# A block projection in forty-two steps instead of eighteen: the turn of queries and keys, one GpSimd operation a step

## The chip, the cores and the metric

The kernel runs on one core of a Trainium2 chip. The metric is the device time of one execution in microseconds. The core's engines are TensorE (PE: matrix products and transposes; PEld: its weight loads), VectorE (DVE), ScalarE (ACT), GpSimd (POOL) and SyncE (SP, which here issues DMA transfers). Each engine works through its own instructions strictly in order and waits on semaphores for what others must deliver.

## The reference

A layer norm, causal attention with rotary positions, and a feed-forward network on the same normalised input whose output gates the attention:

```python
xn = _layernorm(x, axis=-1)                     # x: (4, 2048, 256)
q, k, v = (split(xn @ W.T + b) for W, b in ...) # 16 heads of 16
q = apply_rope(q); k = apply_rope(k)            # x * cos + rot(x) * sin
att = jnp.einsum('bhqd,bhkd->bhqk', q, k) / scale
att = jnp.where(mask, att, -jnp.inf)            # causal
y = softmax(att) @ v                            # per head, then joined
s = y @ Wo.T + bo
h = gelu(xn @ ternary(W1).T + b1)               # 1024 wide
g = silu(h @ ternary(W2).T + b2)
out = x + s * g
```

## The kernel before

The 4 x 2048 rows are cut into 16 *blocks* of 512 rows (`NB`), four to a sequence; `n = blk % 4` is a block's place in its sequence. For each block there are four stages: `project` (layer norm, transposes, queries, keys and values), `feed` (the feed-forward network), attention, and `finish` (output projection, gate, residual).

Attention goes over 64 *groups*: a block and four of its sixteen heads. Within a group the generator `values` runs over *units*, one for each 128 keys that the block may see, so a group has 4 (n + 1) units: 4, 8, 12 or 16. A unit computes scores on TensorE (L791), their exponential on ScalarE (L798) and the product with the values on TensorE (L815); the product of one unit is issued in the second half of the next. The last four units of a group lie on the diagonal: there GpSimd zeroes the masked triangle with two selects (L802), and the value product waits for them. The value products of a group's last two units are issued only after the first unit of the next group (`end`). `maxima` computes the row maxima of the *next* group (L704 on TensorE, L727 and L731 on VectorE) between the units of this one.

The order of instructions on every engine is written out by hand: the main loop (L1092 to L1146) calls these generators in turn, and each engine's queue holds what was issued in that order. Side work goes between the units. A generator is wrapped in `Paced`, which knows how many steps it has and, called with a share, runs as many as this share asks for. After each unit the loop advances the projection of a later block:

```python
proj, p0, p1 = Paced(project(b2), [1] * N_Q), g, g + over   # L1105
proj.to(1.05 * (g + (u + 1) / units - p0) / (p1 - p0))       # L1137
```

So a projection is spread over two groups. Which block is projected where says `beside` (L1053): while n = 1 or 2 is attended, the next block is projected in groups 0 and 1; while n = 3 is attended, the next block in groups 0 and 1 and the one after in groups 2 and 3; while n = 0, none. Blocks 0 and 1 are projected during the start (`start` is true for them, and VectorE does their arithmetic in place of GpSimd); the other fourteen are projected as described. Before a block is fed (`feed`, begun in the middle of the group ahead of the one named in `hids`) its projection is finished in one go if it isn't yet (`proj.rest()`, L1133). `feed` starts with four GpSimd operations on the transposed input (`split`, L572), and its `hl` differences (L594) are GpSimd's too.

The steps of `project`, each ended by a `yield`, are before the change: four steps of statistics on VectorE (L411, L412), of which the fourth also issues the normalisation on GpSimd (L419 to L432 on four columns, then L444 and L447 on the whole block); three more steps with nothing in them; two steps of four transposes (L455) and a copy (L458); then the query pair in two steps (two matmuls at L513 and an activation at L521 each), the key pair likewise, four steps of value products (L539, L548), and the store of the values. With the first query step go the load of the next block's x (L402) and of the rotation table cos_sin (L470), both on SP. As soon as a pair stands, `turn` (L474) rotates it: six multiplications, additions and subtractions of 128 x 512, and two calls of `split` (L391), which write a number as a sum of a rounded part and a rest (two operations each). These ten operations, all on GpSimd, are issued in one go, ahead of the key pair's first matmul or, for the keys, ahead of the first value product; the four stores of a turned pair to DRAM (L502, on SP) follow them. The tiles `qkhi`, `qklo`, `r0`, `r1` and `cos_sin` exist once each, `qk0` and `qk1` twice. `N_Q` (L1038) counts the steps: 18.

Of the kernel before, what the change touches and what calls it, by code (L numbers as in the profile page):

```python
# [20 lines left out]
NB = 512  # L21
# [17 lines left out]
def attention_gated_by_ffn(  # L39
# [40 lines left out]
    NT = T // P  # L80
    QK = 2 * D
    PR = H // 2

    x_blk = x.rearrange("b (n t p) d -> (b n) p t d", t=TT, p=P)
    out_blk = out.rearrange("b (n t p) d -> (b n) p t d", t=TT, p=P)
# [305 lines left out]
    def split(hi, lo, full, width):  # L391

        z = zero
        for _ in width[1:]:
            z = z.unsqueeze(1)
        nc.gpsimd.tensor_tensor(hi, full, z.to_broadcast([P, *width]), ALU.add)  # L396
        nc.gpsimd.tensor_tensor(lo, full, hi.bitcast(F32), ALU.subtract)  # L397


    def load(blk):  # L400
# [3 lines left out]
    def project(blk):  # L404
# [12 lines left out]
        start = blk < 2  # L417
# [25 lines left out]
        else:  # L443
# [1 line left out]
                xn, xn, mv[:, :, 0:1].to_broadcast([P, TT, D]), ALU.subtract  # L445
            )
            eng.tensor_tensor(xn, xn, r.unsqueeze(2).to_broadcast([P, TT, D]), ALU.mult)  # L447
        for _ in range(4):
            yield

        xf = x_T[blk] = tp.tile([P, KC, NB], F32, tag="tT", name="xf")
# [22 lines left out]
        def turn(i, t0, t1):  # L474
            r0 = one.tile([P, NB], F32, tag="r0", name="r0")
            r1 = one.tile([P, NB], F32, tag="r1", name="r1")
            eng.tensor_tensor(r0, t0, cos, ALU.mult)
            eng.tensor_tensor(r1, t1, sin, ALU.mult)
            eng.tensor_tensor(r0, r0, r1, ALU.subtract)
            if not start:  # L480
                split(hi[:, 2 * i, :], lo[:, 2 * i, :], r0, (NB,))
            else:
                nc.scalar.copy(hi[:, 2 * i, :], r0)
            eng.tensor_tensor(t0, t0, sin, ALU.mult)
            eng.tensor_tensor(t1, t1, cos, ALU.mult)
            eng.tensor_tensor(t0, t0, t1, ALU.add)
            if not start:
                split(hi[:, 2 * i + 1, :], lo[:, 2 * i + 1, :], t0, (NB,))
            else:
                nc.scalar.copy(hi[:, 2 * i + 1, :], t0)  # L490
                for k, full in ((2 * i, r0), (2 * i + 1, t0)):
                    eng.tensor_tensor(
                        lo[:, k, :], full, hi[:, k, :].bitcast(F32), ALU.subtract
                    )

            dd, rows = ((qd, (hi, hi, lo, lo)), (kd, (hi, lo, hi, lo)))[i]
            for c, src in enumerate(rows):
                to = dd[blk].rearrange(
                    "r (a f s c) k -> c (r a f) s k", a=2, f=HF, s=2
                )  # L500
                queue = nc.scalar if blk == 0 and i == 1 else nc.sync
                queue.dma_start(  # L502
                    out=to[c], in_=src[:, 2 * i : 2 * i + 2, :].bitcast(F32)
                )

        pairs = []
        for i in range(2):
            pair = []
            for s in range(2):
                pq = bank("pq")  # L510
                for kc in range(KC):
                    at = (2 * i + s) * P
                    nc.tensor.matmul(  # L513
                        pq,
                        wqkvT[:, kc, at : at + P],
                        xf[:, kc, :],
                        start=(kc == 0),
                        stop=(kc == KC - 1),
                    )
                t = work.tile([P, NB], F32, tag=f"qk{s}", name=f"qk{s}")  # L520
                nc.scalar.activation(t, pq, AF.Identity, bias=bqk[:, i, s : s + 1])  # L521
                release("pq")
                pair.append(t)
                yield
            pairs.append((i, *pair))
            while pairs and (blk or i):
                turn(*pairs.pop(0))


        v = one.tile([P, TT, VW], F32, tag="v", name="v")  # L530
# [35 lines left out]
    def feed(blk):  # L566

        xf = x_T.pop(blk)
        xh = tp.tile([P, KC, NB], F32R, tag="tT", name="xh")
        xl = tp.tile([P, KC, NB], F32R, tag="tT", name="xl")  # L570
        for kc in range(KC):
            split(xh[:, kc, :], xl[:, kc, :], xf[:, kc, :], (NB,))  # L572
        yield
        gate = gs[blk] = work.tile([P, KC, NB], F32, tag="g", name=f"g_{blk}")
        pgs, halves = [bank(f"pg{dc}") for dc in range(KC)], {}
        for f in range(FC + 2):
            if f < FC:
                ph = bank("ph")
                for kc in range(KC):
                    for i, x12 in enumerate((xh, xl)):  # L580
                        nc.tensor.matmul(  # L581
                            ph,
                            w1T[:, kc, f * P : (f + 1) * P],
                            x12[:, kc, :],
                            start=(kc + i == 0),
                            stop=(kc + i == KC),
                        )
                h = work.tile([P, NB], F32, tag="h", name="h")
                hh = hp.tile([P, NB], F32R, tag="hh", name="hh")
                hl = hp.tile([P, NB], F32R, tag="hl", name="hl")  # L590
                for to in (hh, h):
                    nc.scalar.activation(to, ph, AF.Gelu, bias=b1c[:, f : f + 1])  # L592
                release("ph")
                nc.gpsimd.tensor_tensor(hl, h, hh.bitcast(F32), ALU.subtract)  # L594
                halves[f] = hh, hl
            yield
            if f >= 2:
                for dc in range(KC):
                    for i, hx in enumerate(halves[f - 2]):
                        nc.tensor.matmul(  # L600
                            pgs[dc],
                            w2T[:, f - 2, dc * P : (dc + 1) * P],
                            hx,
                            start=(f - 2 + i == 0),
                            stop=(f - 2 + i == FC),
                        )
        for dc in range(KC):
            nc.scalar.activation(  # L608
                gate[:, dc, :], pgs[dc], AF.Silu, bias=b2c[:, dc : dc + 1]
            )  # L610
            release(f"pg{dc}")
        yield
# [423 lines left out]
    CHUNK, BESIDE, SH, END = 200, 300, 0.5, -200  # L1036
    N_R = 1 + 2 * 2 * (NQ - 1) + 2 * (1 + 12)
    N_Q = TT - 1 + 4 + KC + 4 + TT + 1  # L1038
    idle = Paced(iter(()), ())

    def max_work(blk):
# [25 lines left out]
    with tc.manual_schedule():  # L1067
# [24 lines left out]
        for i, (blk, g) in enumerate(groups):  # L1092
            n = blk % NQ
            units = (n + 1) * TT
            loads.now = i
            loads.go()
            nxt = groups[i + 1] if i + 1 < len(groups) else None
            maxs = Paced(maxima(*nxt), max_work(nxt[0])) if nxt else idle
            projs, hids = beside(blk)
            if g in projs:  # L1100
                proj.rest()
                b2, over = projs[g]
                proj = idle
                if b2 < NBLK:
                    proj, p0, p1 = Paced(project(b2), [1] * N_Q), g, g + over  # L1105

            fast = hids.get(g, NBLK) < NBLK
            slots = [CHUNK] * FC if fast else []
            for u in range(units):
                w = NB - max(u - n * TT, 0) * P  # L1110
                w += 80 + (BESIDE if proj is not idle else 0)
                slots += [w * SH, w * (1 - SH)]
            whole = sum(slots[:-2]) - END
            past = 0
            if fast:
                for k, _ in enumerate(gate):
                    past += slots.pop(0) if k < FC else 0

                    if k % 3 == 2:
                        maxs.to(past / whole)  # L1120
            steps = values(blk, g)
            for u in range(units):
                past += slots.pop(0)
                maxs.to(past / whole)
                next(steps)
                past += slots.pop(0)
                maxs.to(past / whole)
                next(steps)
                if u == 0 and ends:
                    ends.pop(0)()  # L1130
                if u == units // 2 and hids.get(g + 1, NBLK) < NBLK:
                    if b2 == hids[g + 1]:
                        proj.rest()  # L1133
                    gate = feed(hids[g + 1])
                    next(gate)
                if proj is not idle:
                    proj.to(1.05 * (g + (u + 1) / units - p0) / (p1 - p0))  # L1137
                if deferred:
                    do = deferred.pop(0)
                    if do:  # L1140
                        do()
            for _ in steps:
                pass
            loads.release("q")
            maxs.rest()
            if g == G - 1:  # L1146
                proj.rest()
# [60 lines left out]
```

## Time and profile before

| | |
|---|---|
| median of 3 runs | 2407.71 us (2400.47 to 2412.79) |
| profiled execution, first to last instruction | 2397.2 us |
| instructions | 43912 |
| selects, L802, GpSimd | 512, 416 ns each, 208.0 us |
| differences of the feed-forward network, L594, GpSimd | 128, 1298 ns each, 164.9 us |
| one operation of a turn, GpSimd (ten rows, 28 of each) | 1041 to 1285 ns |
| normalisation of a whole block, L444 and L447, GpSimd | 1898 and 1895 ns |
| row maxima, L727, VectorE | 2048, 666 ns each, 1258.2 us |
| exponentials, L798, ScalarE | 1280, 894 ns each, 1081.3 us |

Times in the profile are microseconds from the first instruction of that execution unless ns is written. A row of a timeline has the start, the duration, the engine, the line of the kernel, the operation, what it writes and reads, the shape and a count of merged instructions; in square brackets stands how long the engine had been idle before it and what released it. A row of waits reads: who waited, for whom, microseconds in all, times, longest. A row of windows has the stretch, its length, the busy time of PE, PEld, DVE, ACT and POOL (with instructions), the clock granted to TensorE as a share of its full speed, the share of the DMA engines' time and GB/s. In the chain of waits, the profile follows the work that ended last back to what released it.

### The profile page before, as it was taken

Reading aid. Unit: us, or ns where it says so; the run is one execution under the profiler, and the core shown is the slowest. Engines: PE = TensorE matmul, PEld = TensorE weight load, DVE = VectorE, ACT = ScalarE, POOL = GpSimd, SP = SyncE. Lnnn points to the kernel's source line nnn. Section 1 sums busy time; section 2 is a strip of 40 time slices with the busy share of each in tenths; the row PEclk is TensorE's granted clock in tenths of the full one; section 3 lists DMA queues with packets and bytes.
Section 4 is the critical chain, followed back from the end, with each engine's and each line's share of the span. In section 5 each row is a group of like instructions: output and inputs, shape, how many; then the busy total and the mean of one; then the engine's idle time right before and its main releaser. Section 6 shows DMA issues by size and latency. Waiting matters only on the chain.

```text
span 2397.2 us, 43912 instructions
## 1 busy us (share of the span) xinstructions
PE 2269.8 (95%) x16852; PEld 1222.7 (51%) x16852; DVE 1620.1 (68%) x2910; ACT 1472.5 (61%) x1889; POOL 886.6 (37%) x1262
## 2 busy tenths in 40 slices
PE   5799999999999999999999999999999999999997
PEld 4554545545455455544545454455554545455443
DVE  9656677775556676696636768768663766777881
ACT  4554656656766565765766565565676646566665
POOL 2136343235443535315344542522525453431000
PEclk8889999999999999999999999999999999999998
DMA  7344335234253524234234443412514352442311
GB/s 222 113 135 161 92 127 157 58 104 136 75 165 118 178 86 159 79 91 145 67 127 128 151 142 111 155 56 86 176 58 140 120 179 79 135 140 62 88 46 32
DMA packets 247617, 280.38 MB, mean 117 GB/s; under 512 B 108784, under 2 KB 143728, under 8 KB 247408
## 3 DMA queue, kind: packets, MB, share of 16 engines
q1 hardware_dynamic: 243680, 271.95, 35.7%
q10 hardware_dynamic: 3728, 5.64, 0.7%
q8 instruction: 132, 2.16, 0.4%
q14 instruction: 77, 0.63, 0.1%
HBM read 181.08 MB, written 87.52 MB: 112 GB/s over the span
## 4 chain that ended last, share of the span: by engine, by line
PE 71%; DVE 10%; ACT 7%; POOL 6%; issue 3%; DMA 2%; SPq 1%; ACTq 0%; DVEq 0%; POOLq 0%
PE psum L791 19%; PE psum L815 19%; PE psum L704 14%; PE psum L600 5%; PE psum L513 3%; PE psum L581 3%; DVE mx L727 3%; ACT e L798 3%; DVE mx L731 2%; PE psum L539 2%; PE psum L953 2%; PE psum L717 2%; ACT mT L765 1%; POOL qklo L397 1%; ACT g L608 1%
## 5 line engine op out<-in xcount | busy, mean ns | idle before, releaser
L727 DVE TENSOR_REDUCE mx<-psum 128x1 f32<-128x512 f32 (+1 forms) x2048 | 1258.2, 666 | 497.1 <-PE psum L704 350.1
L798 ACT ACTIVATE e<-psum 128x1024 f32<-128x1024 f32 (+3 forms) x1280 | 1081.3, 894 | 630.4 <-PE psum L791 596.0
L704 PE MATMUL psum<-kst,qst 64*128 64x512 f32 (+3 forms) x2560 | 613.0, 421 | 27.1 <-ACT h L592 9.3
L815 PE MATMUL psum<-e,vg 128*32 128x512 f32 (+3 forms) x5120 | 596.5, 543 | 15.7 <-POOL e L802 15.5
L802 POOL TENSOR_SCALAR_AFFINE_SELECT e<-e 128x256 f32<-128x256 f32 x512 | 208.0, 416 | 1001.0 <-ACT e L798 972.2
L791 PE MATMUL psum<-qst,kst 64*128 64x512 f32 (+3 forms) x2560 | 554.6, 395 | 22.3 <-DVE mx L727 5.7
L704 PEld LDWEIGHTS psum<-kst,qst 64*128 64x128 f32 x2560 | 309.0, 185 | 449.4 <-DVE mx L727 287.9
L791 PE MATMUL psum<-mT,sel 64*128 64x512 f32 (+3 forms) x2560 | 516.8, 370 | 6.0 <-ACT mT L765 3.2
L791 PEld LDWEIGHTS psum<-qst,kst 64*128 64x128 f32 x2560 | 285.1, 185 | 171.9 <-ACT e L798 55.4
L791 PEld LDWEIGHTS psum<-mT,sel 64*128 64x128 f32 x2560 | 273.3, 186 | 43.7 <-ACT mT L765 24.1
L594 POOL TENSOR_TENSOR hl<-h,hh 128x512 fp32r<-128x512 f32 x128 | 164.9, 1298 | 149.9 <-ACT h L592 114.3
L815 PEld LDWEIGHTS psum<-e,vg 128*32 128x32 f32 x5120 | 109.9, 108 | 161.0 <-issue 112.4
L731 DVE TENSOR_REDUCE mx<-psum 128x3 f32<-128x384 f32 x256 | 130.3, 552 | 57.7 <-PE psum L717 53.3
L592 ACT ACTIVATE hh<-psum,b1c 128x512 fp32r<-128x512 f32 x128 | 88.4, 691 | 80.4 <-PE psum L581 80.2
L513 PE MATMUL psum<-xf,wqkvT 128*128 128x512 f32 x256 | 125.9, 616 | 0.9 <-ACT xf L458 0.9
L717 PE MATMUL psum<-mask_k,mask_q 64*128 64x64 bf16 (+1 forms) x1536 | 121.1, 205 | 0.0
L600 PE MATMUL psum<-hh,w2T 128*128 128x512 f32 x256 | 107.1, 418 | 0.2 <-ACT w2T L367 0.2
L581 PE MATMUL psum<-xh,w1T 128*128 128x512 f32 x256 | 104.8, 409 | 0.6 <-POOL xh L396 0.5
L581 PE MATMUL psum<-xl,w1T 128*128 128x512 f32 x256 | 103.1, 403 | 0.8 <-POOL xl L397 0.8
L600 PE MATMUL psum<-hl,w2T 128*128 128x512 f32 x256 | 102.3, 399 | 0.2
L521 ACT ACTIVATE qk<-psum,bqk 128x512 f32<-128x512 f32 x64 | 44.0, 689 | 86.4 <-PE psum L513 85.9
L592 ACT ACTIVATE h<-psum,b1c 128x512 f32<-128x512 f32 x128 | 87.9, 687 | 0.0
(135 smaller groups left out, 1635.9 us busy)
## 6 DMA issues: line engine op xcount, KB each, us to landing
kst<-kd SPq DMA_DIRECT2D x160, 512.0 KB
qst<-qd SPq DMA_DIRECT2D x64, 512.0 KB
vg<-vd SPq DMA_DIRECT2D x160, 166.0 KB
qd<-qkhi SPq DMA_DIRECT2D x32, 512.0 KB
qd<-qklo SPq DMA_DIRECT2D x32, 512.0 KB
kd<-qkhi SPq DMA_DIRECT2D x30, 512.0 KB
kd<-qklo SPq DMA_DIRECT2D x30, 512.0 KB
vd<-v SPq DMA_DIRECT2D x16, 574.0 KB
```

The lines of the kernel that those rows point to most:

```text
L513: nc.tensor.matmul(pq, wqkvT[:, kc, at : at + P], xf[:, kc, :], start=(kc == 0), stop=(kc == KC - 1),)
L581: nc.tensor.matmul(ph, w1T[:, kc, f * P : (f + 1) * P], x12[:, kc, :], start=(kc + i == 0), stop=(kc + i == KC),)
L592: nc.scalar.activation(to, ph, AF.Gelu, bias=b1c[:, f : f + 1])
L600: nc.tensor.matmul(pgs[dc], w2T[:, f - 2, dc * P : (dc + 1) * P], hx, start=(f - 2 + i == 0), stop=(f - 2 + i == FC),)
L704: nc.tensor.matmul(s1[:, at : at + wt], q[rows, j, t * P : (t + 1) * P], kst[blk, g, c][rows, j, :wt], start=(at == 0), stop=(c < n),)
L717: nc.tensor.matmul(to[:, :, i * ST : (i + 1) * ST], mask_q[rows, i, :], mask_k[rows, i, : len(ts), :], start=False, stop=(i == 1),)
L727: nc.vector.tensor_reduce(mx[:, 2 * j + a, at : at + 1], s1[:, :w], AX.X, ALU.max)
L731: nc.vector.tensor_reduce(mx[:, 2 * j + a, at : at + w // P], s1[:, :w].rearrange("p (b k) -> p b k", k=P), AX.X, ALU.max,)
L791: nc.tensor.matmul(s2[:, a, :w], (k, sels[j][rows, :])[part], (q[rows, j, q0:], mT[rows, q0:])[part], start=(part == 0), stop=(part == 1),)
L798: nc.scalar.activation(e, s2[:, :, :w], AF.Exp, scale=1.0 / math.sqrt(HD))
L802: nc.gpsimd.affine_select(out=e[:, :, :P], in_=e[:, :, :P], pattern=[[0, 2], [1, P]], compare_op=ALU.is_ge, fill=0.0, base=0, channel_mult ...
L815: nc.tensor.matmul(av[h * HP : (h + 1) * HP, q0:], vst[blk, g, kb // TT][:, kb % TT, h * VE : h * VE + HP], ex[h // 2][:, h % 2, : NB - q0 ...
```

## The change

`split` and `turn` become generators that yield after each operation, so a turn is issued in ten steps in place of one go; `feed` runs `split` through without a pause as before. At the start (blocks 0 and 1) `turn` yields nowhere. The empty steps after the normalisation become eight in place of four yields (`N_W`). The count of a projection's steps rises from 18 to 42 (`N_T` is 20 + 4), over the same two groups.

```diff
+    N_W = 8
...
         nc.gpsimd.tensor_tensor(hi, full, z.to_broadcast([P, *width]), ALU.add)
+        yield
         nc.gpsimd.tensor_tensor(lo, full, hi.bitcast(F32), ALU.subtract)
+        yield
...
-        for _ in range(4):
+        for _ in range(4 if start else N_W):
             yield
...
+            apart = () if start else (None,)
             eng.tensor_tensor(r0, t0, cos, ALU.mult)
+            yield from apart
             eng.tensor_tensor(r1, t1, sin, ALU.mult)
+            yield from apart
             eng.tensor_tensor(r0, r0, r1, ALU.subtract)
+            yield from apart
             if not start:
-                split(hi[:, 2 * i, :], lo[:, 2 * i, :], r0, (NB,))
+                yield from split(hi[:, 2 * i, :], lo[:, 2 * i, :], r0, (NB,))
             else:
                 nc.scalar.copy(hi[:, 2 * i, :], r0)
             eng.tensor_tensor(t0, t0, sin, ALU.mult)
+            yield from apart
             eng.tensor_tensor(t1, t1, cos, ALU.mult)
+            yield from apart
             eng.tensor_tensor(t0, t0, t1, ALU.add)
+            yield from apart
             if not start:
-                split(hi[:, 2 * i + 1, :], lo[:, 2 * i + 1, :], t0, (NB,))
+                yield from split(hi[:, 2 * i + 1, :], lo[:, 2 * i + 1, :], t0, (NB,))
...
-                turn(*pairs.pop(0))
+                yield from turn(*pairs.pop(0))
...
-            split(xh[:, kc, :], xl[:, kc, :], xf[:, kc, :], (NB,))
+            for _ in split(xh[:, kc, :], xl[:, kc, :], xf[:, kc, :], (NB,)):
+                pass
...
+    N_T = 2 * 2 * (3 + 2) + N_W - 4
...
-                    proj, p0, p1 = Paced(project(b2), [1] * N_Q), g, g + over
+                    proj, p0, p1 = Paced(project(b2), [1] * (N_Q + N_T)), g, g + over
```

## The prediction

> **What bounds the kernel now.** I read the page first: engine shares, then the chain of waits.
>
> ```profile
> span 2397.2 us, 43912 instructions
> ...
> PE 2269.8 (95%) x16852; PEld 1222.7 (51%) x16852; DVE 1620.1 (68%) x2910; ACT 1472.5 (61%) x1889; POOL 886.6 (37%) x1262
> ...
> PE 71%; DVE 10%; ACT 7%; POOL 6%; issue 3%; DMA 2%; SPq 1%; ACTq 0%; DVEq 0%; POOLq 0%
> ```
>
> TensorE is the bound: 95% busy, 127 us idle, of which windows of 100 us put 33 into the first (67.2 busy) and 16 into the last 97 (81.3 busy). Work that GpSimd does costs time only where TensorE stops for it. So the second view is who TensorE waited for:
>
> ```profile
> PE psum L815 <- POOL e L802: 15.5, 12, 1.5
> ```
>
> Twelve stops for a select (L802) that came late, 15.5 us in all: this is the most that GpSimd's order can give back directly. The third view is the timeline of a block with n = 1 (block 5, 16 units in its first two groups), GpSimd first:
>
> ```profile
> 759.66 0.23 POOL L419 TENSOR_SCALAR var<-mv 128x4 f32<-128x4 f32 x1 [10.40 <-DVE mv L412]
> ...
> 765.47 1.90 POOL L447 TENSOR_TENSOR xn<-xn,r 128x1024 f32<-128x1024 f32 x1
> 767.32 1.49 POOL L802 TENSOR_SCALAR_AFFINE_SELECT e<-e 128x256 f32<-128x256 f32 x4
> ...
> 778.60 1.27 POOL L477 TENSOR_TENSOR r<-qk,cos_sin 128x512 f32<-128x512 f32 x1 [3.92 <-DMA cos_sin<-cs]
> ...
> 804.48 1.27 POOL L397 TENSOR_TENSOR qklo<-qk,qkhi 128x512 fp32r<-128x512 f32 x1
> ...
> 805.87 1.49 POOL L802 TENSOR_SCALAR_AFFINE_SELECT e<-e 128x256 f32<-128x256 f32 x4
> ```
>
> The four selects at 767.32 stood behind the normalisation (L419 to L447, 7.7 us from 759.66), those at 805.87 behind both turns, which run back to back from 778.60. TensorE in the same stretch:
>
> ```profile
> 761.10 1.07 PE L815 MATMUL psum<-e,vg 128*32 128x512 f32 x8
> 762.09 0.50 PE L704 MATMUL psum<-kst,qst 64*128 64x512 f32 x2
> ...
> 767.78 1.41 PE L815 MATMUL psum<-e,vg 128*32 128x512 f32 x8 [1.02 <-POOL e L802]
> 769.12 0.66 PE L455 MATMUL psum<-ident,xn 128*128 128x128 f32 x4
> ...
> 777.81 0.86 PE L815 MATMUL psum<-e,vg 128*32 128x256 f32 x16
> ...
> 806.33 1.41 PE L815 MATMUL psum<-e,vg 128*32 128x512 f32 x8 [1.50 <-POOL e L802]
> ```
>
> The first stop costs 1.0 us, the second 1.5. Both recur in each of the four blocks with n = 1. The third kind of stop (1.38 us, four times) stands behind feed's splits of xf, which the change leaves. In blocks with n = 2 and 3 no stop of over 1 us occurs: their turns fall on units without selects. Last, the windows of the second group of blocks 1, 5, 9, 13, the same work four times:
>
> ```profile
> 196.90:236.40 39.50, 37.17 (x238) 19.07 (x236) 23.34 (x39) 16.48 (x23) 27.47 (x30) 0.96 0.53 190
> 776.00:813.90 37.90, 35.53 (x240) 18.52 (x236) 23.31 (x39) 16.48 (x23) 27.56 (x30) 1.00 0.55 197
> 1353.50:1391.40 37.90, 35.58 (x240) 18.59 (x236) 23.32 (x39) 16.53 (x23) 27.55 (x30) 1.00 0.56 198
> 1931.30:1970.70 39.40, 37.07 (x240) 19.06 (x236) 23.52 (x39) 16.58 (x23) 27.55 (x30) 0.96 0.54 192
> ```
>
> In two of the four the clock (the column after GpSimd's) dropped after the 1.5 us stop, and the group took 1.5 us longer (39.45 against 37.9). A stop can cost its length and 1.5 us more.
>
> **The change, part by part.** No instruction is added or removed; 280 turn operations of some 1.24 us (346 us over their ten rows) stay on GpSimd. What changes is the step count, 18 to 42, and so the place of every step of a projection. The pace is 1.05 times the share of units done: for n = 1, 1.18 steps a unit before and 2.76 after; n = 2, 0.79 and 1.84; n = 3, 0.59 and 1.38.
>
> *Removed, n = 1.* The fourth statistic comes after the second unit, not the third, so the normalisation ends some 2.5 us earlier, and before the first select is ready: 4 x 1.02 = 4.1 us back. In the built order not twenty turn operations in one run stand ahead of unit 13's select, but twelve handed out over units 8 to 12, the last seven after the tenth: 7 x 1.28 = 9 us against three units of 2.9 us and a unit's grace: 4 x 1.46 = 5.9 us back. With them go the two slow stretches, 2 x 1.5 = 3.0. Sum 13.0.
>
> *Added, n = 1: the transposes of xn.* Steps after the normalisation are 8 now, but a unit takes 2.76 of them: the first four transposes stand after the fourth unit, where TensorE is at 762.1 in the rows above, and not after the sixth (769.1). The fourth statistic runs on VectorE right after the second unit's four reduces. With one more statistic ahead of them that is 756.6 (third statistic now at 756.02, plus 0.55), the normalisation starts at 757.2 and ends 7.7 later, at 764.9. TensorE, delayed 0.2 by VectorE, stands from 762.3: 2.65 us. The bounds are 2.3 (statistic at 756.02) and 2.9 (no delay). TensorE is in order, so scores, maxima and all else queue behind these transposes. 4 x 2.65 = 10.6. Per block the normalisation's cover was 1.8 us of slack (767.37 to 769.12); it is gone.
>
> *Added, n = 1: the first turn falls on units 7 and 8.* Its first operation needs cos_sin, which came 5.2 us after its issue (773.42 to 778.60). Counting on from the transposes at 765.0: unit 5 2.85, second transposes 0.65 (cos_sin asked for at 769.6, there at 774.8), projection 1.98, unit 6 3.1, projection 1.98, so 776.1; its activation 776.8; the second operation ends at 778.1; unit 7's selects at 779.4, three operations 3.7, unit 8's selects 0.8: 784.0. TensorE needs unit 7's and 8's selects only after the first unit of the next group (the x16 row): 776.1 + 2.6 + 0.9 + 2.5 = 782.1, and unit 8's 0.4 later. That is a stop of 1.5; since the sum takes every unit at full length on TensorE and GpSimd's waits at their shortest, the ends are 0 and 2.5, and I take 1.0: 4.0 us. The value products of the next group, and so everything, queue behind it.
>
> *Added, n = 2 and 3.* For n = 2 the selects of units 9 to 12 now alternate with two operations: 2 x 1.28 + 0.83 = 3.4 us a unit. Such units start 2.8, 2.7, 2.1 and 1.6 us apart (block 6, between first matmuls of L791) where nothing else lies in them; two output products of 0.95 us lie after units 11 and 12. Unit 9's select ends 3.7 after its start, unit 12's then 3.7 + 3 x 3.4 = 13.8; TensorE asks for it after 9.2 + 1.9 + 2.4 + 0.4 = 13.9. Late by 0 to 0.7 as these add up; I take 0.2: 4 x 0.2 = 0.8. For n = 3 one or two operations lie between: 0.
>
> *The clock.* Three of three pauses of 3.1 to 3.5 us in the first 120 us were followed by a lower clock (windows there: 0.80, 0.73, 0.76), two of four of 1.46, none of eight at 1.0 to 1.4. For 2.65 I take three of four, 3 x 1.5 = 4.5, between 0 and 9 (all, and two of the 1.0 stops). The Trainium skill (TensorE: Matmul & The Clock Gate, What's actually happening) lets the clock fall after an idle window of about 3.4 us; by that rule a 2.65 us pause would cost nothing more and the sum would be 4.5 lower. The rows at 1.46 us speak against it, so the rows decide.
>
> *Hidden.* Steps of DMA keep their order on SP's queue but for x and cos_sin, now ahead of rd and rw for n = 1: rw is used some 8 us after it lands, so 3.5 us late is covered; without cover it would be 3.5 a block. The turn's stores wait on SP for less time than before. VectorE's yT product took 1.30 and 1.13 us beside a turn (779.12, 783.44) against 0.69 median, and for n = 2 it now meets the turn: 8 x 0.6 us at most on an engine 68% busy; 0.
>
> The Trainium skill (SBUF — State Buffer, SBUF: two separate sides) says a two-input VectorE operation and a GpSimd one exclude each other for a whole instruction. The slow yT rows agree; by its rule up to 1.3 us could be lost at each of the eight, which the sum would still put on VectorE.
>
> Sum: -13.0 + 10.6 + 4.0 + 0.8 + 4.5 = +6.9 us on the profiled 2397.2, so a span of 2404. The median of the runs is 10.5 above that span, the lowest 3.3; the median plus 6.9 is 2414.6, and I say 2415. With all low ends: -13 + 9.2 = -4. With all high ends: -13 + 11.6 + 10 + 2.8 + 9 = +20.
>
> **Rivals.**
> *Hidden after all.* VectorE or GpSimd is earlier than I count, the transposes wait 1 us or less, no clock drop follows, and the old stops are merely swapped for shorter ones: 4 x 1.0 + 4 x 1.0 - 13 = -5, up to +2; 2403 to 2410. For it: 2.65 is a difference of two modelled times. Against: the order is fixed and the normalisation's 7.7 us is the same in every block.
> *Faster: only the old stops go.* The mechanism is normalisation and selects both coming ahead of TensorE. It decides if the transposes come 2.65 us later than I have them, or the normalisation is that much earlier. Then all 13.0 are kept: 2407.7 - 13.0 = 2394.7. Against it stand the four-unit row; for it, that nothing else on the list is above 1.0 a block.
> *Slower: the backlog of GpSimd.* The selects of three units fall late in every n = 2 projection (4 x 3 x 1.5 = 18 us, two operations' 2.6 less 1.1 of grace) and of one unit for n = 3 (6 x 1.5 = 9), on top of 6.9: +34, 2441. For it: 3.4 against 1.6 to 2.8 us. Against: the last two selects of a group are not needed for another unit, and GpSimd catches up there.
>
> **How the numbers follow.** Forecast (+2 to +20) 0.58, hidden (-5 to +2) 0.18, faster 0.10, backlog 0.14. The forecast's own range is 2410 to 2428; the range 2401 to 2430 takes in hidden and leaves out the faster case and most of the backlog. About 0.5%, 12 us, is what a measurement of this kernel can tell from no change. Of the forecast 0.22 lies above +12; with the backlog, slower 0.36. Half of the faster case (-13 is near the bound) counts as faster: 0.05. The rest, 0.59, is the same.
>
> **What would show it.** In the changed profile: L815's wait for the select without the 1.5 stops before unit 13; a new wait of 2 to 3 us of the transposes for GpSimd's xn, four times, at the fourth unit of n = 1; a stop of about 1 us in the first unit of the next group. I am wrong if the xn wait is under 1 us, if n = 2 blocks lengthen by over 2 us, or if n = 3 blocks change at all.

## The result and the profile after

The changed kernel takes 2428.71 us (median of 5 runs, 2426.08 to 2430.01) against 2408.05 before: a ratio of 1.0082, 95% interval 1.0058 to 1.0106. The changed kernel is about 20 us slower. Its profiled execution is 2427.0 us long. The head of its page:

```profile
span 2427.0 us, 43916 instructions
...
PE 2284.6 (94%) x16852; PEld 1230.7 (51%) x16852; DVE 1631.9 (67%) x2910; ACT 1475.1 (61%) x1889; POOL 888.5 (37%) x1262
...
PE 75%; DVE 10%; ACT 7%; issue 3%; DMA 3%; POOL 3%; SPq 0%; ACTq 0%; DVEq 0%; POOLq 0%
```

GpSimd's part of the chain that ended last fell from 6 to 3%, which is what spreading its work was meant to do, and yet the span grew by 30 us. TensorE is idle for 142 us where it was 127, and busy for 15 us longer with the same 16852 matmuls. Busy time that grows with nothing added means slower matmuls, and the granted clock is indeed 0.976 in the mean, after 0.986. (The 30 us are more than the 20 of the medians because the profiled execution of before was its quickest, 2400.47; the 29 runs of that kernel beside the first experiments go from 2399.33 at a clock of 0.986 to 2419.04 at 0.981.)

What TensorE waited for in the changed kernel (who, for whom, microseconds, times, longest):

```profile
PE psum L768 <- DVE m_pad L759: 21.4, 43, 1.2
...
PE psum L715 <- DVE mx L738: 10.2, 17, 3.2
PE psum L458 <- POOL xn L450: 10.1, 4, 2.5
...
PE psum L715 <- DVE mx L742: 9.0, 7, 3.4
...
PE psum L826 <- POOL e L813: 6.2, 4, 1.6
```

The same three rows of VectorE in the kernel before:

```profile
PE psum L757 <- DVE m_pad L748: 12.8, 33, 0.8
...
PE psum L704 <- DVE mx L727: 4.7, 5, 3.2
...
PE psum L704 <- DVE mx L731: 3.5, 7, 0.9
```

The wait for selects (L826, once L815) went from 15.5 us in twelve stops to 6.2 in four, which are feed's. A new one of 10.1 us in four stops has come: transposes for xn. The wait for m_pad (the row maxima as a tile that TensorE reads at the start of a group) grew from 12.8 to 21.4, that of the row maxima's matmuls for mx from 8.2 to 19.2. Of the latter 6.5 us are three stops in blocks with n = 0, where nothing is projected. The second of the four new stops, with what follows it (timeline of TensorE, block 5, n = 1):

```profile
769.33 1.07 PE L826 MATMUL psum<-e,vg 128*32 128x512 f32 x8
772.92 1.11 PE L458 MATMUL psum<-ident,xn 128*128 128x128 f32 x4 [2.53 <-POOL xn L450]
...
777.25 1.93 PE L826 MATMUL psum<-e,vg 128*32 128x512 f32 x8
```

Four transposes take 1.11 us where they took 0.66, and the same eight products 1.93 where the row above has 1.07: after the stop the engine runs at half speed. The windows of that stretch say so (the clock is the third figure from the end):

```profile
770.00:773.00 3.00, 0.47 (x5) 0.08 (x2) 0.53 (x1) 0.29 (x1) 2.79 (x2) 0.95 0.42 145
773.00:779.50 6.50, 6.50 (x34) 3.29 (x35) 3.04 (x5) 2.52 (x3) 0.81 (x2) 0.50 0.00 1
779.50:790.00 10.50, 9.93 (x80) 5.06 (x78) 4.83 (x10) 5.22 (x9) 4.95 (x7) 1.00 0.51 157
```

For 6.5 us TensorE is fully busy at a clock of 0.50. GpSimd meanwhile had normalised as fast as ever, only with nothing to hide behind:

```profile
765.20 0.23 POOL L422 TENSOR_SCALAR var<-mv 128x4 f32<-128x4 f32 x1 [8.04 <-DVE mv L415]
...
770.98 1.89 POOL L450 TENSOR_TENSOR xn<-xn,r 128x1024 f32<-128x1024 f32 x1
```

From 765.20 to 772.87 are 7.7 us, as before; the transposes were asked for at 770.4.

### The profile page after: what moved, and what is told of

Same layout as the page of the kernel before. It is cut to its first block, busy times and chain, and to the rows that moved or that the text cites. A ratio compares the mean times of both kernels' runs of the same rounds, so it can differ in the third digit from the quotient of the medians.

```text
span 2427.0 us, 43916 instructions
## 1 busy us (share of the span) xinstructions
PE 2284.6 (94%) x16852; PEld 1230.7 (51%) x16852; DVE 1631.9 (67%) x2910; ACT 1475.1 (61%) x1889; POOL 888.5 (37%) x1262
## 4 chain that ended last, share of the span: by engine, by line
PE 75%; DVE 10%; ACT 7%; issue 3%; DMA 3%; POOL 3%; SPq 0%; ACTq 0%; DVEq 0%; POOLq 0%
PE psum L802 20%; PE psum L826 19%; PE psum L715 14%; PE psum L611 5%; PE psum L523 5%; PE psum L592 4%; DVE mx L738 3%; ACT e L809 2%; PE psum L549 2%; PE psum L964 2%; DVE mx L742 2%; PE psum L728 2%; ACT mT L776 1%; ACT g L619 1%; PE psum L768 1%
## 5 line engine op out<-in xcount | busy, mean ns | idle before, releaser
L715 PE MATMUL psum<-kst,qst 64*128 64x512 f32 (+3 forms) x2560 | 603.2, 421 | 36.0 <-DVE mx L738 10.2
L826 PE MATMUL psum<-e,vg 128*32 128x512 f32 (+3 forms) x5120 | 597.2, 546 | 7.0 <-POOL e L813 6.2
L802 PE MATMUL psum<-qst,kst 64*128 64x512 f32 (+3 forms) x2560 | 564.5, 402 | 19.3 <-ACT e L809 5.6
L802 PE MATMUL psum<-mT,sel 64*128 64x512 f32 (+3 forms) x2560 | 522.3, 373 | 4.7 <-ACT mT L776 0.4
L826 PEld LDWEIGHTS psum<-e,vg 128*32 128x32 f32 x5120 | 109.3, 109 | 157.4 <-issue 114.7
```

The costliest lines, as they stand in the source:

```text
L715: nc.tensor.matmul(s1[:, at : at + wt], q[rows, j, t * P : (t + 1) * P], kst[blk, g, c][rows, j, :wt], start=(at == 0), stop=(c < n),)
L802: nc.tensor.matmul(s2[:, a, :w], (k, sels[j][rows, :])[part], (q[rows, j, q0:], mT[rows, q0:])[part], start=(part == 0), stop=(part == 1),)
L826: nc.tensor.matmul(av[h * HP : (h + 1) * HP, q0:], vst[blk, g, kb // TT][:, kb % TT, h * VE : h * VE + HP], ex[h // 2][:, h % 2, : NB - q0 ...
```

## The experiments

Theory "cover": the loss sits in the four projections made while n = 1 is attended, where the transposes now come two units after the normalisation, and in the clock that falls behind those stops. Rival "spread": side work on other units in all fourteen projections costs TensorE time, whatever happens at the transposes. All times are medians; ratios are to the kernel before on the same chip. The expectations are in microseconds, counted from 2408; on the chips of the experiments the kernel before took 2405 to 2411, so the ratios are the safer measure. The changed kernel itself was measured beside the first result only.

**One empty step more.**

```diff
-    N_W = 8
+    N_W = 9
```

> Theory 'cover' (the loss sits in the n = 1 projections: TensorE stands four times 2.5 us for xn, and the clock drops behind it): one empty step more puts the transposes after the fifth unit of n = 1 in place of the fourth, a unit of 2.9 us later, so the wait of the transposes for xn falls from 10.1 us to under 1, the half-clock stretches that follow it go too, and the kernel takes 2411 to 2418 us against 2408 before and 2429 changed. Rival 'spread' (the loss comes from side work that lies on other units in all fourteen projections, VectorE waits and late selects): the wait goes, but the time stays at 2420 or above, as the waits for m_pad and mx take its place.

Measured: 2406.33 us, ratio 0.9982 (0.9964 to 0.9999). One empty step takes back the whole loss. By the step arithmetic the share of 45.15 / 16 = 2.82 steps a unit puts the thirteenth step behind the fifth unit, where 2.76 put the twelfth behind the fourth. The transposes of block 5 in this kernel (timeline of TensorE):

```profile
765.12 1.06 PE L826 MATMUL psum<-e,vg 128*32 128x512 f32 x8
766.12 1.09 PE L458 MATMUL psum<-ident,xn 128*128 128x128 f32 x8
767.45 1.98 PE L523 MATMUL psum<-xf,wqkvT 128*128 128x512 f32 x4 [0.24 <-ACT xf L461]
```

No stop for xn and no half clock; all eight transposes now fall in one unit, and the projection's first matmul waits 0.24 us for the copy. The wait for m_pad stayed at 21.5 us, so that is not the main thing that made the kernel slow. "Cover" holds, "spread" falls as the main cause. The range expected was missed on the quick side by 5 us (8, against the kernel before on that chip).

**The old four empty steps at the new pace.**

```diff
-    N_W = 8
+    N_W = 4
```

> N_W = 4, the old number of empty steps with the new pace: the transposes stand after the third unit of n = 1. 'Cover': the wait for xn grows by one unit, 2.5 + 2.9 = 5.4 us each, 21 us in all, and the kernel takes 2438 to 2446 us. 'Spread': what is lost at the transposes is given back in the units behind them, where VectorE has caught up; 2425 to 2433.

Measured: 2445.76 us, 1.0147 (1.0123 to 1.0171), inside "cover". The four stops are 5.7 us each (22.8 us in the list of waits). Nothing is given back behind them.

**One empty step fewer.**

```diff
-    N_W = 8
+    N_W = 7
```

> N_W = 7, one empty step fewer. By the step arithmetic the transposes stay behind the fourth unit of n = 1. 'Cover' (whole units count): the wait for xn stays at 10 us and the time at 2424 to 2432. If the empty steps count one by one: the wait grows by a third of a unit, 4 us in all, 2433 to 2438.

Measured: 2434.74 us, 1.0098 (1.0081 to 1.0115). The wait for xn is 10.2 us in four stops, as with eight: it goes by whole units. The time does not decide: 2434.74 us is in the range of the second expectation, but on a chip where the kernel before takes 2408.97, and 1.0098 of 2408 is 2432, the end of the first. Its interval overlaps that of the change (to 1.0106), so whether the seventh step itself costs something is not told apart; the wait for m_pad is 27.9 us here.

**One part alone: which projections.** The steps for n = 1 only, then for all others only:

```diff
+        stepwise = not start and (blk % NQ == 2)     # second kernel: blk % NQ != 2
-        for _ in range(4 if start else N_W):
+        for _ in range(N_W if stepwise else 4):
...
-                yield from turn(*pairs.pop(0))
+                if stepwise:
+                    yield from turn(*pairs.pop(0))
+                else:
+                    for _ in turn(*pairs.pop(0)):
+                        pass
...
-  Paced(project(b2), [1] * (N_Q + N_T))
+  Paced(project(b2), [1] * (N_Q + N_T * (b2 % NQ == 2)))   # second: != 2
```

> Only the four projections during n = 1 are in forty-two steps, the other ten as before the change. 'Cover': nearly the whole loss, 2423 to 2430 us. 'Spread': four of fourteen parts of it, 2412 to 2417.

Measured: 2420.35 us, 1.0038 (1.0023 to 1.0054). In microseconds that is between the two theories; against the kernel before on that chip it is a loss of 9 us, the upper end of "spread" (4 to 9) and not "cover" (15 to 22).

> The complement: the four projections during n = 1 as before the change, the other ten in forty-two steps. 'Cover': 2406 to 2413 us, no wait of the transposes for xn. 'Spread': ten of fourteen parts of the loss, 2420 to 2425.

Measured: 2414.03 us, 1.0014 (0.9997 to 1.0031): a loss of 3 us on that chip, inside "cover" (-2 to 5) and far below "spread" (12 to 17). So each half speaks against one theory, and neither holds alone. Together the two give 0.52% of the 0.82%; the three intervals are wide enough to allow that. Three quarters of what the parts show is made by four projections in fourteen.

Where the time lies can be read from the profiles. Each value is the time from the first exponential of a block to that of the next (of the last block, to its last), summed over the four blocks of one n; the last column is the time at half clock in the blocks with n = 1:

| kernel | n = 0 | n = 1 | n = 2 | n = 3 | half clock, n = 1 |
|---|---|---|---|---|---|
| before | 273.1 | 521.5 | 676.9 | 808.6 | 6.8 |
| changed | 279.8 | 537.3 | 676.8 | 813.7 | 41.0 |
| N_W = 9 | 275.3 | 510.6 | 676.3 | 818.4 | 6.8 |
| steps for n = 1 only | 281.3 | 535.6 | 677.1 | 809.0 | 37.5 |
| steps for all but n = 1 | 275.7 | 527.5 | 676.8 | 814.9 | 23.9 |

Of the 30 us between the two profiles, 16 lie in n = 1, 5 in n = 3, none in n = 2 and 7 in n = 0. The code for n = 0 is the same in both kernels, so these 7 us show what chance does to one profile; a stop for mx of 3.4 us stands there also in the kernel before with the early feed, further below. Of the 16 us some 6 may be chance too, since the kernel in the last row, whose n = 1 is as before, takes 527.5. For n = 3 there is no such doubt: the four kernels that project there as before take 808.6 to 809.0, and all eight with single steps or the new pace 813.7 to 835.7. TensorE's wait for m_pad in these blocks is 2.1 us before and 5.8 after. So most of the loss is n = 1, which is "cover", and some 5 us are "spread", in n = 3 alone.

**The clock by itself.** TensorE is given useless work in place of the stop:

```diff
             pt = bank("pt")
+            if not start and blk % NQ == 2 and kc == 0:
+                for _ in range(6):
+                    nc.tensor.matmul(
+                        pt, w1T[:, 0, :P], w1T[:, 0, :NB], start=True, stop=True
+                    )
```

> The changed kernel with six matmuls of 128x512 (some 0.4 us each, their result is overwritten) ahead of the first transposes of the n = 1 projections, so that TensorE works through the 2.5 us in which it stood for xn. Nothing else moves. Theory 'clock': the stop cost more than its length, because the granted clock fell behind it in four of four; with the engine busy the half-clock stretches behind it go and the kernel takes 2418 to 2425 us, though no wait was removed. Rival: the length alone counts; 2426 to 2432 us.

Measured: 2414.68 us, 1.0027 (1.0015 to 1.0039), quicker than "clock" had it. Work was added, nothing that TensorE waits for comes earlier, and the kernel is 13 us quicker than the change (0.0055 of 2408; by the intervals 7 to 20). Block 5 again, first TensorE, then the windows:

```profile
767.31 1.66 PE L459 MATMUL psum<-w1T 128*128 128x512 f32 x6
769.94 0.66 PE L463 MATMUL psum<-ident,xn 128*128 128x128 f32 x4 [0.97 <-POOL xn L450]
...
772.45 1.07 PE L831 MATMUL psum<-e,vg 128*32 128x512 f32 x8
```

```profile
767.00:770.00 3.00, 2.03 (x11) 1.11 (x8) 0.51 (x1) 0.27 (x1) 2.81 (x2) 1.00 0.43 152
770.00:776.50 6.50, 6.50 (x50) 3.58 (x52) 3.08 (x6) 3.67 (x5) 0.82 (x2) 1.00 0.11 30
```

The transposes still come 2.6 us late (1.66 of filler and 0.97 of stop), but the clock stays at 1.00, and in the 6.5 us behind them TensorE does 50 matmuls where the change did 34. So of the 24 us between the change (1.0082) and N_W = 9 (0.9982) some 13 were clock and, by this kernel's 1.0027, some 11 the length of the stops. In the blocks with n = 1 the clock is at a half for 3.4 us here and for 41.0 in the change.

**The pace without the split.** The steps stay where the change puts them, but each turn is issued in one go:

```diff
-                yield from turn(*pairs.pop(0))
+                for _ in turn(*pairs.pop(0)):
+                    pass
+                if not start:
+                    yield
...
-  Paced(project(b2), [1] * (N_Q + N_T))
+  Paced(project(b2), [1] * (7 + N_W) + [10, 1, 1, 10] + [1] * 5)
```

> The pace of the change for every step (same units for statistics, transposes, matmuls and value products), but each turn in one go, at the place of its first operation. If the split into single operations does what its place asks, selects now stand behind up to ten operations, 12.4 us, on the diagonal units of n = 1, 2 and 3: stops of some 6 us in four, 9 us in four and 6 us in six projections, 2490 to 2530 us. If single steps bring nothing and only the pace counts: 2424 to 2434.

Measured: 2552.58 us, 1.0594 (1.0573 to 1.0614), more than expected. Its waits:

```profile
PE psum L829 <- POOL e L816: 90.4, 18, 9.2
PE psum L718 <- DVE mx L741: 28.7, 19, 5.0
```

The stops are 6.6 us for n = 1, 9.2 for n = 2 and, in three of six projections, 5.7 for n = 3, as counted from ten operations; behind them VectorE was left with a backlog (28.7 us) and the clock fell further, which was not in the count. At these places single steps are worth over 120 us; they avoid what the new pace would otherwise have caused.

**Taking away feed's stops too.** With N_W = 9 the remaining stops for selects stand behind feed's splits, in the diagonal of n = 1:

```diff
-    N_W = 8
+    N_W = 9
...
-  if u == units // 2 and hids.get(g + 1, NBLK) < NBLK:
+  if u == units // 2 - 2 * (n == 1) and hids.get(g + 1, NBLK) < NBLK:
```

> N_W = 9, and feed's four splits two units earlier where n = 1, ahead of the diagonal. The four stops of 1.37 us for selects behind these splits go, with what clock drops follow them: 5 to 8 us under the kernel with N_W = 9, 2398 to 2403 us. If such stops are hidden by what follows: 2405 to 2409.

Measured: 2397.85 us, 0.9949 (0.9933 to 0.9966): quicker than either kernel, at the quick end of what was expected. The wait for selects is 0.6 us, after 6.0 with N_W = 9 alone.

The same line in the kernel before, alone:

> The kernel before, with feed's splits two units earlier where n = 1 and nothing else. If what the kernel with N_W = 9 and the early feed gained (0.51% under before) comes from feed alone: 0.4 to 0.5% under before, 2397 to 2400 us, and the single steps bring nothing. If the steps bring their share, the removed stops of 1.0 and 1.46 us: 0.2 to 0.3% under before, 2401 to 2404.

Measured: 2400.54 us, 0.9979 (0.9966 to 0.9993). Feed alone brings 0.2%, so the single steps with nine empty ones bring some 0.3% of their own by this difference, and 0.2% where they were measured alone (0.9982).

And the steps for n = 1 only, with N_W = 9 and the early feed:

> Single steps only during n = 1, N_W = 9, early feed; the ten projections during n = 2 and 3 as before the change. If the steps for n = 2 and 3 cost the 3 us that were measured for them alone, this takes 2394 to 2397 us, 0.6% under before; if that was noise, the same 2397 to 2400 as with all in single steps.

Measured: 2389.42 us, 0.9936 (0.9922 to 0.9949), the quickest here. The microseconds are below the range expected, but the ratio is the 0.6% that was expected if the steps for n = 2 and 3 cost time. Its list of TensorE's waits has no row of L831 (the value product) for selects any more; the largest rows:

```profile
PE psum L773 <- DVE m_pad L764: 18.4, 41, 1.1
PE psum L344 <- ACT w1T L349: 10.9, 3, 7.8
```

Its interval and that of all projections in steps (up from 0.9933) overlap, so the times alone do not settle that the steps for n = 2 and 3 cost something (0.14% alone, 0.13% here). The profiles do, for n = 3: 809.0 us in these blocks here, 818.4 with all in steps. The run also answers an objection to N_W = 9, which moves the steps of all projections: against the kernel with the steps for n = 1 only and N_W = 8 (1.0038) it gains 1.0%, of which the early feed gave 0.2 to 0.3% elsewhere. The rest, some 0.7%, comes from the four projections of n = 1 alone.

## Why the prediction was right

The forecast was 2415 us, 2401 to 2430, for this reason: stops for selects go and stops for xn take their place. The mechanism is what the runs show; the number lies inside the range with some luck. Against 2407.71 the change is +21.0 us, three times the +6.9 of the sum and just beyond its high end of +20 (2428); only the two microseconds that the range has above that take 2428.71 in. Step by step:

- *Removed, n = 1:* 4 x 1.02 and 4 x 1.46 us, 9.9 in all. Measured: 15.5 to 6.2, that is 9.3. The slow stretches that would go with them did not, since others came.
- *Transposes of xn:* 4 x 2.65 = 10.6. Measured 10.1, four stops of 2.53, in the unit that was named. Taking the cover back (N_W = 9) and taking more of it away (N_W = 4, 5.7 us each) show it from both sides.
- *Unit 8's selects under the first turn:* 4.0 predicted. In block 5 they ended at 793.58, just after TensorE asked (the products at 792.88 took 1.16 us in place of 0.86): 0.3 us, and the same in block 13; in blocks 1 and 9 the products took 1.51, at half clock. TensorE had itself lost time in between, to the half clock and to m_pad, and so asked later. The stop of 1.17 us in this unit is for m_pad, not for a select.
- *n = 2:* 0.8 predicted; the groups of n = 2 take 3.1 us more in the first and 3.1 less in the second, 0.0 in all, in each of the four blocks. No stop there.
- *n = 3:* 0 predicted, 5 us measured by the table, of which 3.7 are TensorE's longer waits for m_pad.
- *The clock* is the term that was mis-sized. For 2.65 us it took "three of four, 3 x 1.5 = 4.5", which is 1.5 net of the 3.0 that would be saved; the run with filler shows some 13. The price of 1.5 us was read from stops of 1.46 us, where one half-clock stretch of 3.4 us followed. The stops of 2.53 us brought such a stretch in four of four, one of them 6.8 us long: 17 of the 41 us at half clock. The other 24 stand behind further stops of the same blocks, four of 1.17 us for m_pad and four of 1.56 behind feed's splits (1.38 before); five of these eight were followed by a stretch within 5 us. The 4.5 of the sum had counted the four stops for xn only. With filler the same eight stops occur, and one was followed by a stretch; why so few is open.
- *VectorE beside GpSimd* was put at 0 because VectorE is not the bound. The rule on the shared port was weighed for the yT product only; the operation that mattered was a smaller one, the cast to m_pad at the end of a group, for which TensorE waits directly. In the changed kernel (VectorE, then GpSimd):

```profile
789.46 0.92 DVE L758 CAST m_pad<-m 128x16 fp32r<-128x16 f32 x1
790.42 0.18 DVE L759 TENSOR_TENSOR m_pad<-m,m_pad 128x16 fp32r<-128x16 f32 x1
```

```profile
789.09 1.26 POOL L485 TENSOR_TENSOR r<-r,r 128x512 f32<-128x512 f32 x1
790.43 1.07 POOL L397 TENSOR_TENSOR qkhi<-r,zero 128x512 fp32r<-128x512 f32 x1
```

  A cast of 16 columns, 0.18 us in the median, takes 0.92 and ends with GpSimd's operation at 790.4; TensorE stood 1.17 us for it. Of the 128 casts and differences into m_pad, 18 took over 0.3 us before and 30 after, each ending within 0.25 us of a GpSimd operation; beyond 0.18 us each that is 7.4 us and 12.5. The Trainium skill (SBUF — State Buffer, SBUF: two separate sides) names a possible reason: a port pair that GpSimd shares with VectorE operations of two inputs or in a two-port mode, and that the one which starts first holds for its whole instruction. The rows agree with it; no run shows in which mode the cast runs. By itself it did not decide: with N_W = 9 the m_pad wait is the same 21.5 us and the kernel is not slower than before.

Of the rivals, "faster" was right about what stood against it: it needed the transposes a unit later, and that one unit is what N_W = 9 gave. "Backlog" would have shown in n = 2 and did not, but it is what happens when the turn is not split at this pace. One of the prediction's own signs of being wrong, "if n = 3 blocks change at all", did come: blocks 3, 7, 11 and 15 changed by +1.7, +2.1, +0.5 and +0.8 us. That is small beside n = 1, but by the table it is no chance; a half-clock stretch lies in the first two (at 533.7 and 1117.4).

## What to carry to other kernels

When side work is handed out by a share of a step count, adding steps moves every step, not only those that were split: list, for each step that waits on another engine, how many units lie between the two before and after, because the cover is a whole number of units and one step can cost or save it. Count a stop of the bounding engine with what its clock does afterwards, and test that with filler work where the engine would stand anyway; here the transposes came 2.63 us late with it and 2.53 without. Spreading an engine's work out takes away long waits behind it, but puts its operations beside short ones of other engines, which can be drawn out by them, as the cast to m_pad was.

## What was not expected of the hardware

TensorE's clock reacted to shorter pauses than thought. Over the twelve profiles of this case (150 to 2350 us), a half-clock stretch began within 5 us of a pause's start in 45 of 49 pauses of over 2.4 us, 9 of 12 of 1.7 to 2.4, 25 of 40 of 1.4 to 1.7, 14 of 63 of 1.0 to 1.4, and 11 of 300 of 0.5 to 1.0. The stretches come in multiples of 3.4 us. The Trainium skill (TensorE: Matmul & The Clock Gate, What's actually happening) names at least one idle window of about 3.4 us as the condition; here pauses well below it were enough.

Runs of one and the same kernel differ together with this clock: the kernel before has 2399.33 us at a mean clock of 0.986 and 2417.96 at 0.980, so a single profile can be a lucky one by 10 us.
